# Moving columns onto VectorE and single lines off SyncE in a graph layer of 400,000 edges

## The chip, the cores and the metric

The kernel runs on one core of a Trainium2 chip. The core has five engines with an instruction stream each: TensorE (PE, products), VectorE (DVE), ScalarE (ACT), GpSimd (POOL) and SyncE (SP), which only issues transfers. The metric is the device time of one execution in microseconds (us); the kernel before takes 3493.72 us, the median of three runs (3492.07 to 3495.51).

An engine's instructions are read by a sequencer, which hands operations to the engine in order. Some instructions are the sequencer's own: loading numbers from memory into registers is one of them (the profile calls it TENSOR_LOAD and marks the sequencer with a q, as in DVEq), and so is issuing a DMA on SyncE.

## What is computed

There are 12,500 nodes with 48 features and 400,000 edges, sorted by their target node `dst`; `src` is random. Every edge also has 32 features of its own.

```
h   = relu(layernorm(x))                                  # 12500 x 48
tmp = concat(h[dst], h[src], edge_attr)                   # 400000 x 128
msg = relu(tmp @ W1 + b1) @ W2 + b2                       # 128 hidden, 48 out
out = x + segment_sum(msg, dst, 12500)
```

All of it is 32-bit.

## The kernel before

**Tables.** The first product is split by its inputs. A first stage of about 100 us (`node_tables`) normalises the nodes and makes two tables in HBM, `tab_a` (for `dst`, with the bias) and `tab_b` (for `src`), 128 numbers a node. It also keeps the second table in on-chip memory with the nodes along the columns: `bt`, 128 partitions by 12,544 nodes.

**Chunks.** The main stage (`windows`) goes through the edges in 391 chunks of 8 tiles of 128 edges (the last one is shorter). As the edges are sorted, the targets of a chunk lie within a window of 80 nodes. For chunk c:

- `prepare` (line 468): SyncE loads one number, the window's first node, and issues three large DMAs: `rhs` (80 rows of `tab_a`, line 474), the edges' features into `lhs` (line 479) and `row`, the targets repeated over 80 partitions (line 481). VectorE makes from `row` the 0/1 matrix in the upper part of `lhs` (line 501) and a second one, `hot` (line 508). `rhs` and `lhs` have three buffers each, and so has `row`.
- `before` (line 514): TensorE multiplies `lhs` by `rhs` into `pre` (line 520): the target's and the edge's part of the hidden layer.
- `gathered` (line 544): VectorE adds the source's part, `gb`, to `pre` and clips at zero: `hid` (line 540).
- `fold` (line 562): TensorE sums the hidden rows by target (line 567) and counts them (line 572) into `p_g`.
- `add` (line 577): VectorE adds `p_g` into a segment of 1,024 nodes, `seg` (line 586).

VectorE thus has four long operations a chunk: `lhs`, `hot`, `hid` and the sum into `seg`. Iteration c of the loop prepares chunk c, multiplies chunk c-1 and folds chunk c-2.

**Three ways for the source's part.** A tile of 128 source rows comes in one of three ways.

1. By gather: GpSimd issues an indirect DMA that fetches the 128 rows from `tab_b` into `gb` (line 490; the buffers are also called `gbl` and `gbs`). Each such gather but a chunk's first waits for one operation of VectorE seven chunks back (`paced`, line 441), so that they are spread over the chunk.
2. By columns: VectorE and ScalarE copy the 128 columns of the tile out of `bt`, one column of 128 numbers an instruction, into a tile `gt` (`columns`, line 420; the copy is line 431). The place of each column is a register that was loaded before. TensorE adds the transposed `gt` to `pre` (line 530).
3. By single lines: SyncE moves the 128 rows of the tile out of `tab_b` one row at a time, 512 bytes a DMA, into a buffer `gbs` (`singles`, line 455; the DMA is line 462). It does this behind the three large DMAs of each chunk, ahead of the next chunk's number and large DMAs, and needs one load of as many numbers first.

**Parts.** How many columns are copied a chunk and by whom is the table `PARTS` (lines 59 to 69): four parts for VectorE and five of 16 for ScalarE. An entry is: VectorE or not, first column, columns, place in `last`, the on-chip array of the numbers. `load` (line 408, its register loads are line 396) loads a part's numbers with one instruction, and `columns` copies them. The order on VectorE in an iteration is written out by hand:

```
lhs;  load 0;  copy 0;  hot;  load 1;  copy 1;
hid;  load 2;  copy 2;  sum into seg;  load 3;  copy 3
```

So each load follows a long operation in the program. Part 0 loads one number more than it has columns, the place of the window in the segment. `BYCOLS` and `BYROWS` (lines 103 and 127) follow from the totals: with 151 columns and 16 lines a chunk, 458 tiles come by columns, 48 by lines and 2,619 by gather. Where a tile is to be complete, and so which chunks get one or two of them, follows from the same totals (`tiles_of`, line 97).

**Segments.** Every 12 chunks the segment changes. SyncE then loads the node rows `xseg` (line 595) and stores the segment before (line 626), with a load of one number each; TensorE multiplies the segment by W2 (lines 616, 617), VectorE adds it to `xseg` in two halves (line 622) and copies the overlap into the next segment (line 606, with a load of one number behind that of part 3), and ScalarE clears the next one (line 600).

## Time and profile before

| | |
|---|---|
| median of three runs | 3493.72 us (3492.07 to 3495.51) |
| profiled execution, its time | 3493.84 us |
| its span, from first to last instruction | 3492.1 us |
| mean granted TensorE clock | 0.776 |
| VectorE busy | 3136.6 us, 90% |
| ScalarE busy | 3172.3 us, 91% |
| TensorE busy (products) | 2656.1 us, 76% |
| GpSimd busy | 2493.5 us, 71% |
| DMA engines' share by queue | 19.4% (GpSimd's), 16.1% (SyncE's) |

Busy time counts an engine's own operations. Register loads, waits and DMA issues are the sequencer's and are not in it; SyncE has nothing else, and is not in the table for that reason. The instructions of an engine overlap by a little: an operation that is listed with 1.21 us may be followed by the next after 1.13 us. What one instruction costs its engine is therefore read from the starts of two that follow each other. A row of the view in order of time gives start, length and the number of like instructions that follow each other; the length reaches from the first one's start to the last one's end. In brackets stands the idle time before them, where it is 0.15 us or more.

A row of the view of one line gives the lengths (shortest, middle, longest, in ns) and the first and the last start in us. A group's row in the view by line gives busy time and mean length, and after the second bar the idle time before these instructions with what ended it; "issue" there is idle time for which the profile shows no waited-for event.

### The profile page before, as it was taken

To read this page: it belongs to the slowest core of one execution; us is meant where nothing else is said; L and a number is where in the kernel's file an instruction comes from. 1 tells how busy PE (TensorE), PEld (TensorE's weight loads), DVE (VectorE), ACT (ScalarE), POOL (GpSimd) and SP (SyncE) were. 2 spreads that over 40 slices of the span, in tenths; PEclk is the share of its full clock that TensorE was granted. 3 is DMA by queue.
4 is the path that set the end of the run, shared out by engine and by line. 5 is a ranking of instruction groups with operands and counts; after the bars stand their busy time and mean duration, and the time that the engine had idled before them with its cause. 6 is when DMAs were issued, how large, how long until landed. Compare 5 with 4: busy or idle time off the path is not lost.

```text
span 3492.1 us, 121785 instructions
## 1 busy us (share of the span) xinstructions
PE 2656.1 (76%) x17111; PEld 2384.2 (68%) x17111; DVE 3136.6 (90%) x29346; ACT 3172.3 (91%) x31179; POOL 2493.5 (71%) x2656
## 2 busy tenths in 40 slices
PE   8577777777778777777777777777778777777777
PEld 6566666666667667676676677666677676667666
DVE  6799999999999999999999999999999999999997
ACT  5999999998999999998999899999999899989893
POOL 5777777777777777777777777777777777777772
PEclk9777777877777777778777777778777777777777
DMA  5533333333333333333333333333333333333332
GB/s 196 168 98 97 95 97 94 97 98 100 96 96 98 96 96 97 95 97 100 96 97 97 97 95 97 95 98 98 98 96 96 97 95 97 97 96 97 96 99 56
DMA packets 199941, 349.44 MB, mean 100 GB/s; under 512 B 69106, under 2 KB 107396, under 8 KB 197844
## 3 DMA queue, kind: packets, MB, share of 16 engines
q0 software_dynamic: 83840, 171.83, 19.4%
q1 hardware_dynamic: 115024, 169.63, 16.1%
q14 instruction: 672, 5.51, 0.5%
q8 instruction: 145, 2.38, 0.3%
q10 hardware_dynamic: 260, 0.10, 0.0%
HBM read 321.82 MB, written 22.07 MB: 98 GB/s over the span
## 4 chain that ended last, share of the span: by engine, by line
DVE 49%; SPq 16%; PE 9%; ACT 9%; DMA 7%; issue 7%; DVEq 3%; ACTq 1%
DVE gt L431 27%; SPq L462 9%; ACT gt L431 8%; DVE lhs L501 8%; DVE hid L540 7%; DMA row<-in_dst 6%; DVE hot L508 5%; SPq L396 4%; DVEq L396 3%; PE p_g L567 3%; PE pre L520 2%; DVE seg L586 1%; PE p_n L241 1%; SPq L479 1%; SPq L474 1%
## 5 line engine op out<-in xcount | busy, mean ns | idle before, releaser
L431 ACT COPY gt<-bt 128x1 f32 x31040 | 3069.6, 187 | 70.0 <-issue 48.2
L490 POOL DMA_INDIRECT gb<-tab_b,srci x1855 | 1750.1, 943 | 669.2 <-issue 379.6
L431 DVE COPY gt<-bt 128x1 f32 x27584 | 1815.8, 144 | 208.9 <-issue 166.4
L567 PE MATMUL p_g<-hot,hid 128*128 128x80 f32 x6250 | 1075.9, 344 | 695.8 <-DVE hid L540 681.4
L567 PEld LDWEIGHTS p_g<-hot,hid 128*128 128x128 f32 x6250 | 1008.4, 253 | 766.6 <-DVE hid L540 751.1
L520 PEld LDWEIGHTS pre<-rhs,lhs 112*128 112x128 f32 x6250 | 974.1, 245 | 199.6 <-issue 127.9
L520 PE MATMUL pre<-rhs,lhs 112*128 112x128 f32 x6250 | 1013.7, 330 | 111.9 <-PE pre L530 48.7
L490 POOL DMA_INDIRECT gbl<-tab_b,srci x476 | 448.9, 943 | 165.6 <-issue 97.9
L501 DVE TENSOR_TENSOR lhs<-row,compared 80x1024 f32<-80x1024 int16 x391 | 472.5, 1209 | 73.7 <-DMA row<-in_dst 71.9
L490 POOL DMA_INDIRECT gbs<-tab_b,srci x288 | 271.7, 943 | 93.6 <-issue 59.8
L540 DVE CUSTOM_DVE_ANT_0 hid<-pre,gb 128x1024 f32<-128x1024 f32 x275 | 333.3, 1212 | 3.6 <-PE pre L530 3.0
L508 DVE TENSOR_TENSOR hot<-compared,rel 128x640 f32<-128x640 f32 x391 | 318.1, 813 | 0.0
L530 PE MATMUL pre<-ident,gt 128*128 128x128 f32 x916 | 274.8, 408 | 5.3 <-issue 4.8
L572 PE MATMUL p_g<-hot,ones 128*128 128x80 bf16 x3125 | 241.9, 239 | 0.0
L572 PEld LDWEIGHTS <-ones 128*128 128x128 bf16 x3125 | 241.8, 133 | 0.0
L530 PEld LDWEIGHTS pre<-ident,gt 128*128 128x128 f32 x916 | 195.9, 273 | 7.4 <-issue 6.1
L600 ACT COPY seg<-nothing 128x944 f32<-128x944 f32 x64 | 62.4, 975 | 151.1 <-PE p_f L616 151.1
L586 DVE TENSOR_TENSOR seg<-seg,p_g 128x160 f32 x391 | 121.2, 310 | 2.2 <-PE p_g L572 2.2
L616 PE MATMUL p_f<-seg,w2s 128*48 128x512 f32 (+1 forms) x134 | 96.4, 812 | 0.8 <-DVE xseg L622 0.8
L540 DVE CUSTOM_DVE_ANT_0 hid<-pre,gbl 128x1024 f32<-128x1024 f32 x68 | 82.6, 1214 | 3.7 <-PE pre L530 3.6
L617 PE MATMUL p_f<-seg,b2s 1*48 1x512 f32 (+1 forms) x134 | 81.5, 691 | 0.0
L617 PEld LDWEIGHTS p_f<-seg,b2s 1*48 1x48 f32 x134 | 11.9, 130 | 78.4 <-issue 77.0
(74 smaller groups left out, 391.4 us busy)
## 6 DMA issues: line engine op xcount, KB each, us to landing
gbs<-tab_b SPq DMA_DIRECT2D x6144, 0.5 KB
row<-in_dst SPq DMA_DIRECT2D x390, 160.0 KB
lhs<-in_edge_t SPq DMA_DIRECT2D x390, 128.0 KB
gb<-tab_b,srci POOLq DMA_INDIRECT x1855
rhs<-tab_a SPq DMA_DIRECT2D x391, 40.0 KB
gbl<-tab_b,srci POOLq DMA_INDIRECT x476
xseg<-in_x_t SPq DMA_DIRECT2D x33, 192.0 KB
out_x<-xseg SPq DMA_DIRECT2D x33, 192.0 KB
```

What stands on the lines that cost most here:

```text
L396: got += nc.values_load_multi_w_load_instructions(last[row : row + 1, slot, at + k : at + min(k + MOST, n)], engines=[engine], min_val=0, ...
L431: done = copy(gts[of][:, e : e + 1], bt8[:, bass.ds(at, 4)].bitcast(F32))
L462: moved = nc.sync.dma_start(to.bitcast(U8)[e : e + 1, :], tabb8[bass.ds(row, 4 * HID)].rearrange("(o h) -> o h", o=1),)
L490: fetch = nc.gpsimd.indirect_dma_start(out=gb[:, t, :], out_offset=None, in_=tab_b[:, :], in_offset=bass.IndirectOffsetOnAxis(ap=srci[:, c ...
L501: mark(nc.vector.tensor_tensor(lhs[:W, : n * P], row[:, : n * P], firsts[:, c : c + 1].to_broadcast([W, n * P]), op=ALU.is_equal,), 1.1)
L508: mark(nc.vector.tensor_tensor(hot[:, :n, :], wnum.unsqueeze(1).to_broadcast([P, n, W]), rel[:, c * T : c * T + n].unsqueeze(2).to_broadca ...
L520: s["behind"] = nc.tensor.matmul(pre[:, t, :], s["lhs"][:K, t * P : (t + 1) * P], s["rhs"][:K, :], start=True, stop=t not in turned_at(c), ...
L530: s["behind"] = nc.tensor.matmul(s["pre"][:, t, :], gts.pop(j), ident, start=False, stop=True).ins
L540: return nc.vector._custom_dve(dve_ops.TENSOR_ADD_SAT, out=to, in0=a, in1=b, s0=float("inf"), s1=0.0)
L567: nc.tensor.matmul(p_g[:, 0, :], s["h"][:, t, :], s["hot"][:, t, :], start=t == 0, stop=t == n - 1)
L572: nc.tensor.matmul(p_g[:, 1, :], ones, high[:, t, 1::2], start=t == 0, stop=t == n - 1)
L586: mark(nc.vector.tensor_add(to, to, s["p_g"]), 0.25)
```

## The change

VectorE's four parts become 19, 20, 24 and 12 columns instead of 23, 20, 20 and 8: 75 a chunk instead of 71. With the one number more of part 0 the loads are of 20, 20, 24 and 12 numbers, behind `lhs`, `hot`, `hid` and the sum into `seg` in this order. ScalarE's five parts of 16 stay. SyncE moves 12 single lines a chunk instead of 16, and loads 12 numbers for them. The places in the array `last` shift accordingly; its width stays.

By the same rules 155 columns a chunk make 471 tiles by columns (13 more), 12 lines a chunk make 36 tiles by lines (12 fewer), and 2,618 tiles are left to the gathers. The chunks that have two tiles by columns are 82 instead of 69.

```diff
 PARTS = (
-    (True, 0, 23, 1),
-    (True, 23, 20, 24),
-    (True, 43, 20, 44),
-    (True, 63, 8, 64),
-    (False, 71, 16, 72),
-    (False, 87, 16, 88),
-    (False, 103, 16, 104),
-    (False, 119, 16, 120),
-    (False, 135, 16, 136),
+    (True, 0, 19, 1),
+    (True, 19, 20, 20),
+    (True, 39, 24, 40),
+    (True, 63, 12, 64),
+    (False, 75, 16, 76),
+    (False, 91, 16, 92),
+    (False, 107, 16, 108),
+    (False, 123, 16, 124),
+    (False, 139, 16, 140),
 )
 PART = sum(n for _, _, n, _ in PARTS)
-BASE = 152
+BASE = 156
 DVE_PARTS = sum(dve for dve, *_ in PARTS)
...
-SEG, NEXT, SEG2 = 153, 154, 155
-PLACE0 = 156
-SINGLE = 16
-SINGLE_AT = 160
+SEG, NEXT, SEG2 = 157, 158, 159
+PLACE0 = 160
+SINGLE = 12
+SINGLE_AT = 164
 WIDTH = 176
```

## The prediction

> **What bounds the kernel now.** I read the page's busy shares first, then the SyncE queue in order of time, then VectorE's waits and its order of time, and last the engines that would be next.

> ```profile
> PE 2656.1 (76%) x17111; PEld 2384.2 (68%) x17111; DVE 3136.6 (90%) x29346; ACT 3172.3 (91%) x31179; POOL 2493.5 (71%) x2656
> ```

> Two engines at 90% invite the guess that one of them is the bound. SyncE is not in that row, because issuing a DMA does not count as busy. Its queue in order of time, its register loads, and line 474 (one a chunk):

> ```profile
> 1681.79 0.32 SPq L474 DMA_DIRECT2D rhs<-tab_a  x1
> ...
> 1690.91 0.32 SPq L474 DMA_DIRECT2D rhs<-tab_a  x1
> ...
> 1700.01 0.32 SPq L474 DMA_DIRECT2D rhs<-tab_a  x1
> ...
> 1700.90 0.36 SPq L481 DMA_DIRECT2D row<-in_dst  x1
> 1702.41 5.16 SPq L462 DMA_DIRECT2D gbs<-tab_b  x16
> 1708.37 0.32 SPq L474 DMA_DIRECT2D rhs<-tab_a  x1
> ...
> 1716.72 0.32 SPq L474 DMA_DIRECT2D rhs<-tab_a  x1
> ```

> ```profile
> L396 SPq TENSOR_LOAD <-last x1: 985/985/985, 1701.3 to 1701.3; - x1
> L396 SPq TENSOR_LOAD <-last x1: 592/592/592, 1707.6 to 1707.6; - x1
> L474 SPq DMA_DIRECT2D rhs<-tab_a x391: 322/322/1062, 96.6 to 3451.8; - x196
> ```

> From 1700.01 to 1708.37 the queue does nothing but issue: three large DMAs, a load of 16 numbers (0.99 us), 16 single lines in 5.16 us (0.32 each), a load of one number, and the next chunk begins. That is 8.36 us, and again 8.35. A chunk with a segment's load (line 595 stands in it) or store takes 9.12 (1681.79 to 1690.91). With two such chunks in twelve: (10 x 8.36 + 2 x 9.12) / 12 = 8.49. The mean is (3451.8 - 96.6) / 390 = 8.60. So SyncE runs back to back and is the bound; VectorE follows it:

> ```profile
> L501 DVE TENSOR_TENSOR lhs<-row,compared x391: 808/1208/1218, 106.8 to 3470.4; 80x1024 f32<-80x1024 int16 x195, 80x640 f32<-80x640 int16 x1
> ```

> ```profile
> DVE gt L431 <- issue: 166.4, 478, 1.1
> DVE lhs L501 <- DMA row<-in_dst: 71.9, 88, 7.5
> ```

> VectorE's period is (3470.4 - 106.8) / 390 = 8.62. It waits 71.9 us for `row` where the gap is long enough to be listed. The larger loss is hidden in "issue", and the order of time shows it (first a chunk whose `row` came late, then one whose `row` was there):

> ```profile
> 1703.78 1.22 DVE L501 TENSOR_TENSOR lhs<-row,compared 80x1024 f32<-80x1024 int16 x1
> 1705.48 1.48 DVE L431 COPY gt<-bt 128x1 f32 x23 [0.49 <-issue]
> 1706.89 0.81 DVE L508 TENSOR_TENSOR hot<-compared,rel 128x640 f32<-128x640 f32 x1
> 1708.02 1.30 DVE L431 COPY gt<-bt 128x1 f32 x20 [0.33 <-issue]
> 1709.24 1.21 DVE L540 CUSTOM_DVE_ANT_0 hid<-pre,gb 128x1024 f32<-128x1024 f32 x1
> 1710.37 1.29 DVE L431 COPY gt<-bt 128x1 f32 x20
> ```

> ```profile
> 1729.12 0.30 DVE L586 TENSOR_TENSOR seg<-seg,p_g 128x160 f32 x1
> 1729.35 0.56 DVE L431 COPY gt<-bt 128x1 f32 x8
> 1729.84 1.20 DVE L501 TENSOR_TENSOR lhs<-row,compared 80x1024 f32<-80x1024 int16 x1
> 1731.26 1.49 DVE L431 COPY gt<-bt 128x1 f32 x23 [0.23 <-issue]
> 1732.66 0.82 DVE L508 TENSOR_TENSOR hot<-compared,rel 128x640 f32<-128x640 f32 x1
> 1733.57 1.51 DVE L431 COPY gt<-bt 128x1 f32 x20
> ```

> ```profile
> L396 DVEq TENSOR_LOAD <-last x1: 1604/1604/1604, 1703.8 to 1703.8; - x1
> L396 DVEq TENSOR_LOAD <-last x1: 1351/1351/1351, 1708.7 to 1708.7; - x1
> L396 DVEq TENSOR_LOAD <-last x1: 607/607/607, 1728.6 to 1728.6; - x1
> L396 DVEq TENSOR_LOAD <-last x1: 1642/1642/1642, 1729.5 to 1729.5; - x1
> ```

> The load of a part's numbers runs beside the long operation in front of it. Where nothing holds that operation, the load starts ahead of it: 0.5 us ahead of `hid` (1708.7 against 1709.24) and of the sum into `seg` (1728.6 against 1729.12), 0.3 us ahead of `lhs` (1729.5 against 1729.84). Where `lhs` had to wait for `row` (issued 2.88 us before it, at 1700.90), the load began only with it, at 1703.8, and the copies came 1.70 us after its start instead of 1.42. Both are more than the 1.13 that an operation of this size takes when nothing is loaded too slowly behind it (`hid`, 1709.24 to 1710.37).

> **The change, part by part.** *SyncE.* It loses four line issues (4 x 0.32 = 1.29 us) and four numbers of a load. A VectorE load of 24 takes 1604 ns and one of 8 607, so a number costs (1604 - 607) / 16 = 62 ns, and four 0.25. Together 1.54 us a chunk: 8.60 falls to 7.06. The three large DMAs of the next chunk then go out up to 1.4 us a chunk earlier, until their three buffers stop them, and `row` is there before VectorE asks. The twelve lines still go out ahead of the next chunk's loads, so nothing is moved past another item on that queue.

> *VectorE, added copies.* 75 instead of 71. From 1708.02 to 1709.24 are 20 copies, 0.061 each: 75 x 0.061 = 4.58 us, of which 0.24 is new, all on the path if VectorE is the bound.

> *VectorE, long operations without stalls.* `lhs` and `hid` 1.13 each; `hot` 0.81 less the 0.08 by which 1.21 exceeds 1.13, so 0.73; the sum 0.23 (1729.12 to 1729.35). Together 3.22.

> *VectorE, stalls behind them.* A copy starts 0.09 us after its load ended (1703.8 + 1.60 = 1705.4, copy at 1705.48). Each stall is head start against load:
> - sum, 12 numbers for 8: the load ended at 1728.6 + 0.61 = 1729.2, the copies could start at 1729.3 and did so at 1729.35, a slack of 0.05 to 0.1 by the rounding. With 0.25 more the stall is 0.15 to 0.20; I take 0.16. This is where the change loses.
> - `lhs`, 20 for 24 (one is the place in the segment): 1.42 less 0.25 is 1.17, a stall of 0.04 to 0.05 against 0.29 now, and against 0.57 where `row` was late.
> - `hot`, 20 as before: 1732.66 to 1733.57 is 0.91, a stall of 0.18; 0.40 in the late chunk. With 19 copies in front instead of 23 the queue builds a little less head start; I take 0.20, ends 0.16 and 0.30 (halfway to the late chunk).
> - `hid`, 24 for 20: load end 1708.7 + 1.35 = 1710.05, plus 0.09 is 1710.14, 0.23 before the copies. With 0.25 more it just fits; I take 0.03, ends 0 and 0.10.

> In all 0.44, ends 0.32 and 0.61.

> ```profile
> L622 DVE TENSOR_TENSOR xseg<-xseg,p_f 48x512 f32<-48x512 f32 (+1 forms) x67 | 44.7, 667 | 4.7 <-PE p_f L617 4.7
> L606 DVE COPY seg<-seg 128x160 f32 x33 | 8.8, 266 | 12.5 <-DVE seg L586 9.5 <-issue 3.0
> ```

> *VectorE, segments and small waits.* 67 x 0.60 (667 ns less the same 0.08, rounded) + 8.8 + 12.5 is 61 us, 0.16 a chunk; waits like the 4.7 listed here, in other places, I put at 0.06 (an estimate, some five times that row).

> Sum: 4.58 + 3.22 + 0.44 + 0.16 + 0.06 = 8.46 us a chunk. Today's arrangement without late rows would be 8.62 less what SyncE causes; the same sum with 71 copies and stalls 0.29 + 0.18 gives 8.24, so SyncE costs 0.38 now. The gain is 8.62 - 8.46 = 0.16.

> *The other engines.* They must stay under 8.46.

> ```profile
> 1701.22 0.95 POOL L490 DMA_INDIRECT gb<-tab_b,srci  x1 [0.30 <-issue]
> 1702.47 0.94 POOL L490 DMA_INDIRECT gb<-tab_b,srci  x1 [0.30 <-issue]
> ...
> L490 POOL DMA_INDIRECT gb<-tab_b,srci x1855: 938/944/1111, 52.2 to 3429.1; - x186
> L490 POOL DMA_INDIRECT gbl<-tab_b,srci x476: 938/944/953, 129.8 to 3422.2; - x159
> L490 POOL DMA_INDIRECT gbs<-tab_b,srci x288: 938/944/967, 122.3 to 3385.8; - x144
> ```

> ```profile
> 1705.29 12.82 ACT L431 COPY gt<-bt 128x1 f32 x128 [0.16 <-issue]
> L600 ACT COPY seg<-nothing x64: 971/976/978, 182.4 to 3396.3; 128x944 f32<-128x944 f32 x64
> ...
> PEld p_g L567 <- DVE hid L540: 751.1, 342, 4.3
> ```

> GpSimd gathers 1855 + 476 + 288 = 2619 tiles, each 1.25 us after the last when nothing waits; 13 tiles more by columns and 12 fewer by lines leave 2618: 2618 x 1.25 / 391 = 8.37, close under 8.46. ScalarE: 80 copies in 12.82 x 80 / 128 = 8.01, clears 64 x 0.976 / 391 = 0.16: 8.17, unchanged. TensorE waits 751 us for `hid`, 1.9 a chunk; 13 tiles more are two products each, 26 over the whole run, and lie in that wait.

> [...]

> **The total.** 390 x 8.46 = 3299.4; the first `lhs` starts at 106.8 and the last at 3470.4 of 3492.1, so 21.7 follow: 3427.9. The profiled execution took 3493.84 for a span of 3492.1, 1.7 more, and lies 0.1 above the median of the runs, 3493.72. That gives 3430 us, 1.8% under the time before.

> **The rivals.**

> *GpSimd holds it up.* Its gathers are paced: each waits for an operation of VectorE some chunks back. 2619 back to back take 3274 us and now fill 52.2 to 3430, so waits make up 104 us, 0.27 a chunk. For: 8.37 is near 8.46, and if half of these waits stay it needs 8.50, that is 390 x 8.50 + 128.5 + 1.7 = 3445. Against: it runs ahead of need (last gather at 3429.1, last `lhs` at 3470.4), and its waits shorten when VectorE is faster.

> *Loads cost less than I take.* If the stalls behind the sum, `lhs` and `hid` vanish, the period is 8.46 - 0.24 = 8.22, 3336 us; but GpSimd then stops it at 52.2 + 2618 x 1.25 + 62 (from its last gather to the end) = 3387, 3388 with the 1.7. Against: 62 ns a number. [...]

> [...]

> *Slower: `row` stays late.* If `row` arrives late for the landing itself (2.88 us from issue to use at 1700.90) and not for SyncE's queue, the lost head start and the waits stay. Then the period gains 0.24 of copies, 0.16 at the sum, 0.05 at `hot` and `hid`, and loses 0.25 at `lhs`: 8.82, and 390 x 0.20 = 78 us more, 3572. It decides once more than half of the 0.38 that SyncE costs now remains. Against: the back-to-back queue; at 1716.72 it begins a chunk 8.35 after the last, as soon as its list is done.

> **How the numbers follow.** Forecast 0.66 (its own range 3400 to 3460: stalls 0.36 to 0.52), GpSimd 0.09, cheaper loads 0.10, no change 0.07, slower 0.08. A measurement of this kernel can tell about 0.2%, 7 us, from no change. Faster: 0.66 + 0.09 + 0.10 = 0.85; same 0.07; slower 0.08. The range runs from 3380, just below the time at which GpSimd stops a faster VectorE, to 3470, stalls of 0.54, near their upper end; the last two rivals lie outside.

> **What would show it.** Right: line 474 no longer back to back, with free time after the twelve lines; no wait of `lhs` for `row`; copies 1.13 to 1.20 us after `lhs` starts; 0.4 us instead of 0.23 from the sum to the copies behind it; `hid` to copies still 1.13 to 1.2. Wrong: `lhs` still held by `row`; gathers over 944 ns, or `hid` waiting for TensorE because gathers are late; a period of line 501 above 8.55.

## The result and the profile after

The changed kernel takes 3455.93 us (median of four runs, 3452.59 to 3458.73) against 3492.89 us (median of four runs of the kernel before): a ratio of 0.9897, with a 95% interval of 0.9879 to 0.9916. That is 37 us or 1.1% faster, where 3430 us (63 us or 1.8% less) was forecast with a range of 3380 to 3470. The profiled execution took 3452.59 us for a span of 3450.8.

Busy shares and the chain that ended last, from the page of the changed kernel:

```profile
PE 2693.3 (78%) x17137; PEld 2378.0 (69%) x17137; DVE 3235.1 (94%) x30937; ACT 3179.9 (92%) x31252; POOL 2499.3 (72%) x2655
DVE 82%; ACT 5%; issue 4%; DVEq 3%; PE 3%; ACTq 0%
```

In the kernel before, the chain that ended last was SyncE's for a sixth and passed through DMAs for another 7%:

```profile
DVE 49%; SPq 16%; PE 9%; ACT 9%; DMA 7%; issue 7%; DVEq 3%; ACTq 1%
```

SyncE has left that chain altogether. Its queue in order of time (start and length in us):

```profile
1602.64 3.92 SPq L462 DMA_DIRECT2D gbs<-tab_b  x12
1615.68 0.34 SPq L626 DMA_DIRECT2D out_x<-xseg  x1
1616.53 0.33 SPq L474 DMA_DIRECT2D rhs<-tab_a  x1
...
1618.70 3.90 SPq L462 DMA_DIRECT2D gbs<-tab_b  x12
1623.35 0.32 SPq L474 DMA_DIRECT2D rhs<-tab_a  x1
...
1630.13 0.32 SPq L474 DMA_DIRECT2D rhs<-tab_a  x1
```

Its waits (us in all, times, longest us):

```profile
SPq L626 <- DVE xseg L622: 332.7, 33, 37.6
SPq L474 <- PE pre L520: 245.3, 78, 8.2
```

A chunk costs SyncE 6.8 us (1616.53 to 1623.35 to 1630.13), and it now has time to wait: 333 us for segments that VectorE has not finished and 245 us for buffers of `rhs`. After the lines at 1602.64 it stands still for 9 us. VectorE's `lhs` and VectorE's waits:

```profile
L501 DVE TENSOR_TENSOR lhs<-row,compared x391: 807/1206/1218, 105.8 to 3424.6; 80x1024 f32<-80x1024 int16 x195, 80x640 f32<-80x640 int16 x1
```

```profile
DVE gt L431 <- issue: 63.5, 207, 3.2
...
DVE lhs L501 <- DMA row<-in_dst: 7.6, 2, 6.5
```

The period is (3424.6 - 105.8) / 390 = 8.51 us instead of 8.62. `lhs` waits for `row` 7.6 us instead of 71.9, and the unexplained idle time before copies fell from 166.4 to 63.5. One chunk of VectorE in order of time, and the three loads in it:

```profile
1632.13 1.22 DVE L540 CUSTOM_DVE_ANT_0 hid<-pre,gb 128x1024 f32<-128x1024 f32 x1
1633.28 1.69 DVE L431 COPY gt<-bt 128x1 f32 x24
1634.88 0.31 DVE L586 TENSOR_TENSOR seg<-seg,p_g 128x160 f32 x1
1635.32 0.82 DVE L431 COPY gt<-bt 128x1 f32 x12
1636.06 1.21 DVE L501 TENSOR_TENSOR lhs<-row,compared 80x1024 f32<-80x1024 int16 x1
1637.18 1.23 DVE L431 COPY gt<-bt 128x1 f32 x19
1638.33 0.81 DVE L508 TENSOR_TENSOR hot<-compared,rel 128x640 f32<-128x640 f32 x1
1639.23 1.30 DVE L431 COPY gt<-bt 128x1 f32 x20
```

```profile
L396 DVEq TENSOR_LOAD <-last x1: 1602/1602/1602, 1631.6 to 1631.6; - x1
L396 DVEq TENSOR_LOAD <-last x1: 847/847/847, 1634.4 to 1634.4; - x1
L396 DVEq TENSOR_LOAD <-last x1: 1350/1350/1350, 1635.7 to 1635.7; - x1
```

`lhs` hides its 20 numbers: 1.12 us to the first copy, no stall. `hid` just holds 24: 1.15 us, where 1.13 is none. Behind the sum the 12 numbers stall: 1634.88 to 1635.32 is 0.44 us instead of 0.23.

### The profile page after: what moved, and what is told of

It reads as the page before. It is cut to its first block, busy times and chain, and to the rows that moved or that the text cites. A ratio compares the mean times of both kernels' runs of the same rounds, so it can differ in the third digit from the quotient of the medians.

```text
span 3450.8 us, 120327 instructions
## 1 busy us (share of the span) xinstructions
PE 2693.3 (78%) x17137; PEld 2378.0 (69%) x17137; DVE 3235.1 (94%) x30937; ACT 3179.9 (92%) x31252; POOL 2499.3 (72%) x2655
## 4 chain that ended last, share of the span: by engine, by line
DVE 82%; ACT 5%; issue 4%; DVEq 3%; PE 3%; ACTq 0%
DVE gt L431 47%; DVE hid L540 12%; DVE lhs L501 11%; DVE hot L508 8%; ACT gt L431 5%; DVEq L396 3%; DVE seg L586 2%; PE p_g L567 1%; DVE xseg L622 1%; PE pre L520 1%; PE p_f L616 0%; PE p_f L617 0%; ACTq L396 0%; PE pre L530 0%; DVE seg L606 0%
## 5 line engine op out<-in xcount | busy, mean ns | idle before, releaser
L431 ACT COPY gt<-bt 128x1 f32 x31113 | 3077.1, 187 | 73.6 <-issue 48.2
L490 POOL DMA_INDIRECT gb<-tab_b,srci x1933 | 1828.5, 946 | 665.6 <-issue 407.0
L431 DVE COPY gt<-bt 128x1 f32 x29175 | 1918.2, 143 | 126.0 <-issue 63.5
L567 PE MATMUL p_g<-hot,hid 128*128 128x80 f32 x6250 | 1046.5, 337 | 545.5 <-DVE hid L540 537.2
L567 PEld LDWEIGHTS p_g<-hot,hid 128*128 128x128 f32 x6250 | 983.0, 247 | 615.2 <-DVE hid L540 606.6
L520 PEld LDWEIGHTS pre<-rhs,lhs 112*128 112x128 f32 x6250 | 985.4, 248 | 255.7 <-issue 156.5
L520 PE MATMUL pre<-rhs,lhs 112*128 112x128 f32 x6250 | 1036.2, 335 | 147.6 <-PE pre L530 72.2
L490 POOL DMA_INDIRECT gbl<-tab_b,srci x469 | 443.7, 946 | 151.9 <-issue 95.5
L501 DVE TENSOR_TENSOR lhs<-row,compared 80x1024 f32<-80x1024 int16 x391 | 471.3, 1205 | 7.6 <-DMA row<-in_dst 7.6
L540 DVE CUSTOM_DVE_ANT_0 hid<-pre,gb 128x1024 f32<-128x1024 f32 x288 | 349.2, 1213 | 2.6 <-PE pre L520 1.8
L508 DVE TENSOR_TENSOR hot<-compared,rel 128x640 f32<-128x640 f32 x391 | 317.3, 812 | 0.0
L490 POOL DMA_INDIRECT gbs<-tab_b,srci x216 | 204.3, 946 | 69.4 <-issue 46.1
L600 ACT COPY seg<-nothing 128x944 f32<-128x944 f32 x64 | 62.4, 974 | 94.5 <-PE p_f L616 91.0
L586 DVE TENSOR_TENSOR seg<-seg,p_g 128x160 f32 x391 | 121.4, 310 | 5.3 <-PE p_g L572 5.3
L616 PE MATMUL p_f<-seg,w2s 128*48 128x512 f32 (+1 forms) x134 | 106.2, 888 | 0.8 <-DVE xseg L622 0.8
L617 PE MATMUL p_f<-seg,b2s 1*48 1x512 f32 (+1 forms) x134 | 94.7, 795 | 0.0
L540 DVE CUSTOM_DVE_ANT_0 hid<-pre,gbl 128x1024 f32<-128x1024 f32 x67 | 81.3, 1214 | 0.2 <-PE pre L530 0.2
L617 PEld LDWEIGHTS p_f<-seg,b2s 1*48 1x48 f32 x134 | 13.1, 144 | 87.4 <-issue 86.6
```

The costliest lines, as they stand in the source:

```text
L431: done = copy(gts[of][:, e : e + 1], bt8[:, bass.ds(at, 4)].bitcast(F32))
L490: fetch = nc.gpsimd.indirect_dma_start(out=gb[:, t, :], out_offset=None, in_=tab_b[:, :], in_offset=bass.IndirectOffsetOnAxis(ap=srci[:, c ...
L501: mark(nc.vector.tensor_tensor(lhs[:W, : n * P], row[:, : n * P], firsts[:, c : c + 1].to_broadcast([W, n * P]), op=ALU.is_equal,), 1.1)
L508: mark(nc.vector.tensor_tensor(hot[:, :n, :], wnum.unsqueeze(1).to_broadcast([P, n, W]), rel[:, c * T : c * T + n].unsqueeze(2).to_broadca ...
L520: s["behind"] = nc.tensor.matmul(pre[:, t, :], s["lhs"][:K, t * P : (t + 1) * P], s["rhs"][:K, :], start=True, stop=t not in turned_at(c), ...
L540: return nc.vector._custom_dve(dve_ops.TENSOR_ADD_SAT, out=to, in0=a, in1=b, s0=float("inf"), s1=0.0)
```

## The experiments

**Theory:** before, SyncE's queue was the bound, and VectorE paid for it twice, in waits for `row` and in lost head start of the loads. Now VectorE is the bound, and its loads' cover decides. **Rivals:** the new split of the parts alone brings the gain; `row` is late for its own landing; GpSimd's gathers hold the changed kernel up.

### SyncE relieved, nothing else

In the kernel before, four of the 16 lines of a chunk are neither loaded nor moved; those rows of the sources' part are left out. Two lines that clear their buffers once at the start are not shown.

```diff
             n = max(0, min(SINGLE, len(BYROWS) * P - (c - COLS) * SINGLE)) if c >= COLS else 0
+            n = min(n, SINGLE - 4)
```

> The kernel before, with its 71 columns in the old split, its tiles and its 2619 gathers, but four of the 16 single lines of each chunk are neither loaded nor moved (those rows of the source's part are left out; the buffers are cleared once at the start). SyncE alone is relieved. Theory (SyncE's queue is the bound before): SyncE falls from 8.60 to 7.06 us a chunk, lhs no longer waits for row, and VectorE runs at 8.24 to 8.30 a chunk: 3350 to 3370 us, unless GpSimd stops it at 8.37 to 8.45: 3390 to 3425. Rival 1 (the new split of the loads brings the gain): no change, 3485 to 3497. Rival 2 (row is late for its own landing): no change, and lhs still waits.

3353.8 us, ratio 0.9599 (0.9583 to 0.9615): 139 us less. In the rows of `lhs` and of the gathers, the line numbers are higher by the three lines added:

```profile
L504 DVE TENSOR_TENSOR lhs<-row,compared x391: 809/1206/1218, 104.8 to 3335.1; 80x1024 f32<-80x1024 int16 x195, 80x640 f32<-80x640 int16 x1
...
L493 POOL DMA_INDIRECT gb<-tab_b,srci x1855: 940/944/1112, 51.3 to 3321.3; - x186
```

The period is 8.28, as the sum for the old arrangement without late rows has it (8.24). Both first rivals fall: the split is the old one, and `row` is in time as soon as SyncE has room (`lhs` waits for it 7.3 us in all, twice, where it was 71.9). GpSimd's stop at 3390, which the expectation kept open, did not come: with 2619 gathers GpSimd ran from 51.3 to 3321.3, (3321.3 - 51.3) / 2618 = 1.249 us each, so back to back over the whole run, and only some 33 us of the span of 3355.6 followed.

### The parts moved, SyncE not relieved

```diff
-SINGLE = 12
+SINGLE = 16
...
-WIDTH = 176
+WIDTH = 180
```

(on the changed kernel; the array of numbers is made wider for the 16)

> The changed kernel with its 75 columns in parts of 19, 20, 24 and 12, but with 16 single lines a chunk as before (2606 gathers, 12 fewer). Theory: SyncE is back to back again at 8.60 us a chunk and sets the time: 3480 to 3500 us, with lhs waiting for row. Rival 1 (the split brings the gain): 3456 or less, since there are fewer gathers too.

3510.94 us, ratio 1.0051 (1.0034 to 1.0068): slower than the kernel before, and 11 us over the range expected. SyncE's queue, line 474 and the chain that ended last in this kernel:

```profile
1623.39 0.32 SPq L474 DMA_DIRECT2D rhs<-tab_a  x1
...
1625.81 5.15 SPq L462 DMA_DIRECT2D gbs<-tab_b  x16
1631.70 0.32 SPq L474 DMA_DIRECT2D rhs<-tab_a  x1
...
L474 SPq DMA_DIRECT2D rhs<-tab_a x391: 322/322/1041, 94.8 to 3464.9; - x196
DVE 74%; SPq 8%; issue 6%; PE 5%; DVEq 3%; DMA 3%; ACT 0%; ACTq 0%
```

The queue is back to back again (8.31 us in a chunk without a segment), and line 474 comes every (3464.9 - 94.8) / 390 = 8.64 us, 8.60 before. So the new split with its four columns gives nothing as long as SyncE keeps its 16 lines; the split with the old 71 columns and 16 lines was not run. But that SyncE alone sets the time here, as the theory had it, is not shown: the chain is VectorE's for 74%, and `lhs` waits for `row` for 17.6 us in all, where it was 71.9 before. VectorE's own time rose too. The copies behind the sum begin 0.46 us after it in the middle of all chunks, where it is 0.39 in the changed kernel: the load of 12 starts 0.49 us ahead of the sum instead of 0.55. On VectorE this costs 0.07 us a chunk, some 26 us in all, and this kernel lies 55 us over the changed one. Why the load starts later was not tested.

### The stall behind the sum taken away

The changed kernel, but the last part loads 8 numbers for 12 columns and uses four of them twice; 4 of 155 columns are then of wrong nodes.

```diff
-nodes = numbers(c, at, n, engine) if n else []
+nodes = numbers(c, at, min(n, 8) if part == 3 else n, engine) if n else []
+nodes = nodes + nodes[: n - len(nodes)]
```

> The changed kernel, but the last part of VectorE loads 8 numbers for its 12 columns and uses four of them twice (4 of 155 columns are then copies of wrong nodes). It takes away the stall of 0.16 us behind the sum into the segment and nothing else. Theory (VectorE is the bound now and that stall is on its path): 8.51 - 0.16 = 8.35 a chunk, 390 x 0.16 = 62 us less, 3394 us; if GpSimd's 8.37 with some of its pacing binds, 3400 to 3430. Rival (the stall lies beside something else that ends later): 3456.

3369.23 us, ratio 0.9652 (0.9633 to 0.9671): 87 us under the changed kernel, more than the 62 expected (3394 us). VectorE in order of time:

```profile
1631.49 0.31 DVE L587 TENSOR_TENSOR seg<-seg,p_g 128x160 f32 x1
1631.72 0.81 DVE L432 COPY gt<-bt 128x1 f32 x12
```

The lines are numbered one higher. The stall is gone (0.23 us), and all of it was on the path. So VectorE is the bound of the changed kernel. It also shows that GpSimd does not hold up the changed kernel: the gathers are the same 2618. The period falls from 8.51 to 8.30. Averaged over the trace from start to start, the time from the sum to the copies accounts for 62 of the 81 us in it, the copy at a segment's change (line 606, whose number's load stands behind that of 12) for 8, and slightly closer copies for 8.

### A middle way, and what a load's place costs

Parts of 19, 20, 24 and 10 with 14 lines:

```diff
-    (True, 63, 12, 64),
-    (False, 75, 16, 76),
+    (True, 63, 10, 64),
+    (False, 73, 16, 74),
...
-SINGLE = 12
+SINGLE = 14
```

> A middle way: parts of 19, 20, 24 and 10 columns (73) and 14 single lines a chunk; 2619 gathers. Theory: SyncE takes 8.60 - 2 x 0.385 = 7.83 us a chunk and is still out of the way; VectorE loses two copies (0.12) and two numbers of stall (0.12): 8.51 - 0.24 = 8.27, 3362 us, or what GpSimd allows at 8.37 to 8.45, 3390 to 3425. Either way faster than the changed kernel. Rival (SyncE needs all four lines taken away): 3456 or more, with row late again.

8007.17 us, ratio 2.2919 (2.2881 to 2.2957). ScalarE's and SyncE's loads in this kernel (lengths in ns), then ScalarE in order of time:

```profile
L396 ACTq TENSOR_LOAD <-last x1940: 3406/3477/4613, 93.6 to 7973.6; - x194
...
L396 SPq TENSOR_LOAD <-last x1: 2872/2872/2872, 4001.6 to 4001.6; - x1
```

```profile
4002.43 1.58 ACT L431 COPY gt<-bt 128x1 f32 x16 [2.39 <-issue]
4006.58 1.58 ACT L431 COPY gt<-bt 128x1 f32 x16 [2.57 <-issue]
```

Nothing of the expectation can be read from it. ScalarE's loads of 16 take 3.4 to 3.5 us instead of 1.02, and every part of 16 columns waits about 2.5 us for its numbers. Their places had moved from 76, 92 and so on to 74, 90: no longer multiples of four words. The same kernel with the places put back to multiples of four:

```diff
-    (False, 73, 16, 74),
+    (False, 73, 16, 76),
...
-SINGLE_AT = 162
-WIDTH = 176
+SINGLE_AT = 164
+WIDTH = 192
```

> The middle way again (19, 20, 24 and 10 columns, 14 lines, 2619 gathers), but every part's numbers now begin at a multiple of four words in their row; two words behind VectorE's last part stay empty. In the run before this one ScalarE's loads of 16 began two words off and took 3.4 us instead of 1.02, SyncE's load of 14 took 2.9, and VectorE's load of 10, which began at a multiple of four, 1.08. Theory A (the place alone makes a load slow): ScalarE's loads take 1.02 us again, VectorE's load of 10 takes 0.73, and the period is 8.51 - 0.24 = 8.27, 3350 to 3375 us. Theory B (a count that is no multiple of four costs too): ScalarE's loads take 1.02, the load of 10 stays at 1.08, the stall behind the sum is 0.40, and the period is 8.51 - 0.12 + 0.21 = 8.60, 3480 to 3500 us.

3521.89 us, ratio 1.0084 (1.0061 to 1.0107). ScalarE's loads are as before, and VectorE's row behind the sum shows the other half:

```profile
L396 ACTq TENSOR_LOAD <-last x56: 1003/1022/1089, 1599.5 to 1698.4; - x56
```

```profile
1627.18 0.31 DVE L586 TENSOR_TENSOR seg<-seg,p_g 128x160 f32 x1
1627.93 0.70 DVE L431 COPY gt<-bt 128x1 f32 x10 [0.45 <-issue]
```

So theory A falls and theory B holds, though the time lies 22 us over its range. 10 numbers, from place 64, a multiple of four, stall 0.75 - 0.23 = 0.52 us behind the sum in the chunk shown, and 0.68 - 0.23 = 0.45 in the middle of all chunks, where 12 stall 0.21 and 0.16. The load of 10 takes 1.09 us here, and those of 12 took 0.85:

```profile
L396 DVEq TENSOR_LOAD <-last x1: 1090/1090/1090, 1626.8 to 1626.8; - x1
```

Here too the load behind the sum starts only 0.49 us ahead of it, as in the kernel with 16 lines; with the 0.55 of the changed kernel the stall would be 0.39, theory B's 0.40, and the time some 25 us less. The place explains the 8007. The count explains most of the 66 us by which this kernel is slower than the changed one with two columns fewer, and the shorter head start, whose cause stays open, the rest.

### Four columns on the old split

The changed kernel with its 75 columns as 23, 20, 20 and 12.

```diff
-    (True, 0, 19, 1),
-    (True, 19, 20, 20),
-    (True, 39, 24, 40),
+    (True, 0, 23, 1),
+    (True, 23, 20, 24),
+    (True, 43, 20, 44),
     (True, 63, 12, 64),
```

> The changed kernel (75 columns, 12 lines, the same tiles and gathers) with the four added columns put on the last part of the old split: 23, 20, 20 and 12. Theory (each load is covered by the operation in front of it or stalls): lhs stalls 0.25 more than in the changed kernel, hid 0.05 to 0.07 less, so 8.51 + 0.19 = 8.70 a chunk, 390 x 0.19 = 74 us more, 3515 to 3540 us: slower than the kernel before. Rival (what was freed at SyncE is all that counts): 3456.

3508.76 us, ratio 1.0043 (1.0022 to 1.0064): slower than before, as expected, but by less than expected: 6 us under the range (the period is 8.67, not 8.70). The row of `lhs` and of the copies behind it:

```profile
1631.37 1.21 DVE L501 TENSOR_TENSOR lhs<-row,compared 80x1024 f32<-80x1024 int16 x1
1632.72 1.49 DVE L431 COPY gt<-bt 128x1 f32 x23
```

1.35 us with 24 numbers against 1.12 with 20. The new split is thus worth 53 us, and without it the change would have lost.

### The four numbers behind `hid`

Parts of 19, 20, 28 and 8.

```diff
-    (True, 39, 24, 40),
-    (True, 63, 12, 64),
+    (True, 39, 28, 40),
+    (True, 67, 8, 68),
```

> The changed kernel with parts of 19, 20, 28 and 8: the four numbers that stall 0.17 to 0.19 us behind the sum go behind hid instead, where 24 just fit. Theory (the cover is used up at hid too): 0.25 of stall at hid against 0.17 to 0.19 saved at the sum, so 8.51 + 0.06 to 0.08, 3475 to 3490 us. Rival (a longer load behind the longest operation is free): 8.51 - 0.19, 3365 to 3385 us.

3458.63 us, ratio 0.9901 (0.9881 to 0.9921): not to be told from the changed kernel, and below the range expected. `hid` and the copies behind it:

```profile
1627.82 1.22 DVE L540 CUSTOM_DVE_ANT_0 hid<-pre,gb 128x1024 f32<-128x1024 f32 x1
1629.20 1.79 DVE L431 COPY gt<-bt 128x1 f32 x28 [0.16 <-issue]
...
1630.91 0.31 DVE L586 TENSOR_TENSOR seg<-seg,p_g 128x160 f32 x1
1631.13 0.57 DVE L431 COPY gt<-bt 128x1 f32 x8
```

The stall moved, from behind the sum (0.22 us to the copies, none) to behind `hid` (1.38, 0.25 over its 1.13). Both places are full, so the rival of a free longer load falls. I had expected 0.25 at `hid` on top of what 24 stall there; on average it grew by 0.20 only, about what the sum saved (0.19).

### A version that beats both

71 columns in the new split and 14 lines, for which 16 numbers are loaded from place 160, a multiple of four. The edit is against the kernel before:

```diff
-    (True, 0, 23, 1),
-    (True, 23, 20, 24),
-    (True, 43, 20, 44),
+    (True, 0, 19, 1),
+    (True, 19, 20, 20),
+    (True, 39, 24, 40),
     (True, 63, 8, 64),
...
-SINGLE = 16
+SINGLE = 14
...
-            for k, row in enumerate(numbers(c, SINGLE_AT, n, mybir.EngineType.SP) if n else ()):
+            for k, row in enumerate(
+                numbers(c, SINGLE_AT, 16, mybir.EngineType.SP)[:n] if n else ()
+            ):
```

> A version that may beat both: the new split with 71 columns (19, 20, 24 and 8, so nothing stalls behind the sum), 14 lines a chunk, for which 16 numbers are loaded from an even place, and the six tiles that are missing by gather (2625). Theory: VectorE 8.30 - 4 x 0.061 = 8.06 a chunk, SyncE 8.60 - 2 x 0.32 = 7.96, ScalarE 8.17, so none of them; GpSimd back to back is the bound: 52 + 2625 x 1.249 = 3331 to its last gather, and 25 to 40 more to the end: 3355 to 3373 us. Rival (GpSimd can't be driven back to back to its end, since a buffer or the pacing stops it): 3390 to 3430.

3352.34 us, ratio 0.9594 (0.9578 to 0.9611): 104 us under the changed kernel, and 3 us under the range expected. `lhs` in two stretches of the run, and TensorE's product with `gt` in the last of them with what it waited for:

```profile
L503 DVE TENSOR_TENSOR lhs<-row,compared x98: 1199/1206/1219, 205.6 to 997.3; 80x1024 f32<-80x1024 int16 x98
...
L503 DVE TENSOR_TENSOR lhs<-row,compared x84: 1201/1206/1217, 2600.8 to 3297.4; 80x1024 f32<-80x1024 int16 x84
```

```profile
L532 PE MATMUL pre<-ident,gt x198: 275/348/562, 2603.8 to 3299.9; 128*128 128x128 f32 x198
...
  DMA gb<-tab_b,srci: 38.8, 19
  DMA gbl<-tab_b,srci: 10.4, 5
```

(Line numbers are two higher here.) VectorE starts at (997.3 - 205.6) / 97 = 8.16 us a chunk and ends at (3297.4 - 2600.8) / 83 = 8.39. GpSimd, back to back all along, needs 2625 x 1.249 / 391 = 8.39: it falls behind until its lead is used up, and then products wait for gathers, 38.8 and 10.4 us of them here. The 8.06 expected of VectorE was 0.10 too low even at the start. Nearly half of that lies behind `lhs`: from its start to the copies it takes 1.20 us on average in the first stretch, 0.05 more than in the same stretch of the kernel without the stall, where only 8 copies stand ahead of it instead of 12 and its load starts 0.30 us ahead of it instead of 0.42 (in the middle of all chunks). The rest is spread over small differences.

## Why the prediction was right, and where it was off

- **The bound before** was SyncE's back-to-back queue, as read: relieving it alone gave 139 us. "SyncE costs 0.38 now" measured 8.62 - 8.28 = 0.34.
- **SyncE after**: 7.06 us was the forecast with segments, and 8.36 - 1.54 = 6.82 by the same working for a chunk without them; it takes 6.8. `row` is there in time; the slower rival fell with the first experiment.
- **The four columns and the split.** The runs put the change together in three steps: relief 3492 to 3354 (139 less), four columns with their numbers on the old split 3354 to 3509 (155 more), the new split 3509 to 3456 (53 less). The first two nearly cancel, and the split decides the sign.
- **The sum, term by term**, by averages from start to start over the whole trace, per chunk. `lhs`: 0.05 forecast, 0.04 measured. `hot`: 0.20 and 0.21. `hid`: 0.03 and 0.07; the 24 numbers just fit in a quiet chunk but not in one with a late or a longer load. Copies: 4.58 plus 0.06 of small waits, and 4.62 with theirs. The sum's stall and segments' work: 0.16 + 0.16, and 0.35, because 12 numbers stall 0.16 in the middle chunk but 0.19 on average, and 0.26 more than before at each of the 33 changes of segment. Together 8.51 for 8.46, or 20 us.
- **Outside the loop**: from the last `lhs` to the end it takes 3450.8 - 3424.6 = 26.2 instead of 21.7, another 4.5 us, which was not followed up. With 1.0 gained at the start, 20 + 4.5 - 1 is the 23 us by which the profiled run (3452.6) lies over the forecast.
- **The mis-sized term** is therefore "In all 0.44", the stalls, at `hid` and behind the sum: they measured 0.04 + 0.21 + 0.07 + 0.17 = 0.49 (the 0.19 behind the sum stand in 355 of 390 chunks), and 0.02 more at the changes of segment; the copies with their small waits gave 0.02 back. The ends that the prediction gives the four stalls add up to 0.35 and 0.65, not to its 0.32 and 0.61; the measured sum lies inside either pair.
- **GpSimd as a rival** was rightly doubted for this kernel: the same gathers served 87 us faster. But "GpSimd then stops it at 3387" was wrong. I kept today's 62 us from the last gather to the end, though that tail is its lead, and a lead can be spent: in the first experiment the span ended 33 us after the last gathers.
- **Cheaper loads** fell: the 0.10 given to them was the author's estimate, and 12 numbers took 847 ns, not the 607 of eight.
- **No change**, given 0.07, was the author's estimate too. No run shows gathers that the four columns make longer by the 0.24 us a chunk which this needed: they take 944 ns with 75 columns of 128 numbers a chunk as with 71 (946 to 947 in the changed kernel's own trace).

```profile
L493 POOL DMA_INDIRECT gbl<-tab_b,srci x476: 940/944/954, 128.9 to 3315.1; - x159
```

```profile
L491 POOL DMA_INDIRECT gb<-tab_b,srci x1933 | 1824.1, 944 | 610.8 <-issue 333.6 <-DVE gt L432 113.2 <-DMA gb<-tab_b,srci 61.3
```

(The first row is of the first experiment with 71 columns, in ns shortest, middle and longest; the second of the one without the stall, with 75, as busy time and mean ns.)

## What to carry to other kernels

SyncE only issues transfers here and had no row among the busy shares, though in the kernel before its queue took 8.60 us for every chunk. Look at such a queue in order of time, and if its chunk begins as soon as the last one's list is done, suspect it as the bound, whatever the busy shares say, and test it by taking work away from it alone. Work taken off it must land on an engine with cover left; here each column beyond the loads' cover costs a copy (0.061 us) and a number's load in the open (some 0.062), and the split of the loads decided between a gain and a loss. GpSimd, which needs 8.39 us a chunk in the last version, let VectorE run at 8.16 at the start, and at 8.39 in the last stretch, when its lead was spent. So compare the total of an engine that runs ahead with the run's, not its rate with a chunk's.

## What the runs showed of the hardware

In the middle of all chunks of the changed kernel a load started 0.55 us ahead of `hot` and `hid`, as long as nine copies of 0.061 take. Ahead of `lhs` it was 0.30 us where 8 copies stood before that (the version that beats both), and with 12 copies 0.34 in the changed kernel and 0.42 in the one without the stall. Behind the part of 8 copies the load thus had 0.25 us less of cover than ahead of `hot` and `hid`.
